# Direct 3x3 convolutions against minimal filtering F(4,3) along the rows, with filters streamed from HBM, in a convolution and attention block on one core

## The chip, the cores and the metric

The kernel runs on one core of a Trainium2 chip, in fp32. The metric is the device time of one launch in microseconds (us). TensorE is called PE in the profile, its weight loads PEld, VectorE is DVE, ScalarE is ACT, GpSimd is POOL and SyncE is SP.

## The reference

For each of 8 batch images of 512 channels x 32 x 32 the reference adds a block of convolutions and attention to the input:

```
t  = cbs(gn(x), cv1_w)            # 1x1, 512 -> 512, split into ys[0], ys[1] of 256 channels
for i in range(2):
    yi = ys[-1]
    z = cbs(yi, m_cv1_w[i])       # 3x3, 256 -> 256, zero padding of 1
    z = attention(z)              # q, k, v by 1x1; k + (rw + rh); softmax over 1024 positions, 4 heads of 64
    ys.append(yi + cbs(z, m_cv2_w[i]))          # 1x1, 256 -> 256
out = x + cbs(concat(ys), cv2_w)                # 1x1, 1024 -> 512
```

`gn` normalises over groups of 16 channels, `cbs` is a convolution, an affine step per channel (evaluation batch norm) and silu.

## The kernel before

Channels lie on the 128 partitions, in chunks of 128 (`NX` = 4 of the input, `NM` = 2 inside the block), and the 1024 positions along the free axis, in two halves of 512. The eight images are worked one after the other by written-out code; the order of the instructions on each engine is set by a scheduler of the framework, which follows the program's order and lets an instruction pass others whose inputs its own model expects later. Each image passes these stages:

- `gn_stats`, `gn_mean` and `gn_apply` (L205 to L238): statistics per channel on DVE, two small matmuls that average over groups, the power -0.5 on POOL (L228), and eight normalising operations on DVE (L233), which write the two `xn` tiles.
- `cv1` (L200 by `conv1x1`): four output chunks of 32 matmuls in the program in all; the first two go to `y0`, the last two to `ypad[0]`.
- `bottleneck(n)` for n = 0, 1: the 3x3 convolution (L432), `project` for q, k and v, `attention_fast`, the 1x1 convolution (L450), silu, and the sum with its input (L462). For n = 0 this sum is written to `ypad[1]`, which the second convolution reads.
- `cv2` (L200): four output chunks, silu, the sum with the input (L481) and the store by POOL's queue (L486).

silu is computed as (tanh(h) + 1) * h, where h is half of the affine step: `silu_parts` does the affine step on DVE out of PSUM (L183) and tanh on ACT (L184), and another DVE operation closes it (L191, L457, L480).

The 3x3 convolution reads `ypad[n]`, a tile with a border of zeros of 34 x 34 per chunk. For each of two output chunks (`oc`), two input chunks (`k`) and nine taps it issues two matmuls of 128 x 512, one per half. The filters `m1_sb` of both bottlenecks lie in SBUF from the start; they are loaded by ACT's queue. A program's fp32 matmul is two matmuls in the trace.

The PSUM pool `ps_big` has 3 tiles of two banks, `ps_av` 2 of one bank. Of the SBUF tag `pt` there are 3 tiles: `xn` and the exponentials of the attention take turns in them.

## Time and profile before

| | us |
|---|---|
| median of 3 runs | 3305.0 (3303.08 to 3305.64) |
| the profiled execution | 3307.59 |
| its span, first to last instruction | 3305.6 |
| PE busy in it | 3168.1 |
| DVE busy | 1490.6 |
| ACT busy | 763.3 |
| mean granted clock of PE in the span | 0.982 |

The busy times are sums over the span. PE's are modelled from the size of a matmul, and matmuls are pipelined; what one costs in a row of many is read from the start of the first and of what follows, over their count. An idle time counts only where the chain of work that ended last runs through it.

### The profile page before, as it was taken

To read this page: it belongs to the slowest core of one execution; us is meant where nothing else is said; L and a number is where in the kernel's file an instruction comes from. 1 tells how busy PE (TensorE), PEld (TensorE's weight loads), DVE (VectorE), ACT (ScalarE), POOL (GpSimd) and SP (SyncE) were. 2 spreads that over 40 slices of the span, in tenths; PEclk is the share of its full clock that TensorE was granted. 3 is DMA by queue.
4 is the path that set the end of the run, shared out by engine and by line. 5 is a ranking of instruction groups with operands and counts; after the bars stand their busy time and mean duration, and the time that the engine had idled before them with its cause. 6 is when DMAs were issued, how large, how long until landed. Compare 5 with 4: busy or idle time off the path is not lost.

```text
span 3305.6 us, 23035 instructions
## 1 busy us (share of the span) xinstructions
PE 3168.1 (96%) x9506; PEld 1303.5 (39%) x9506; DVE 1490.6 (45%) x1746; ACT 763.3 (23%) x961; POOL 57.3 (2%) x116
## 2 busy tenths in 40 slices
PE   6999999999999999999999999999999999999997
PEld 3434344343443434434444343443334333343333
DVE  2353633536335463444524455253552536516264
ACT  0222202222022320313103131031410404104040
POOL 1000000000000000000000000000000000000000
PEclk9999999999999999999999999999999999999999
DMA  4000000000000010000100001000010000100000
GB/s 154 1 0 0 26 26 0 0 0 26 26 0 0 0 37 14 0 0 1 38 13 1 0 0 39 13 0 0 1 51 1 0 0 0 45 0 0 0 0 27
DMA packets 14639, 45.23 MB, mean 14 GB/s; under 512 B 3264, under 2 KB 3776, under 8 KB 14016
## 3 DMA queue, kind: packets, MB, share of 16 engines
q1 hardware_dynamic: 4608, 16.78, 2.1%
q0 software_dynamic: 5632, 16.82, 1.3%
q10 hardware_dynamic: 4288, 10.09, 0.8%
q8 instruction: 77, 1.26, 0.2%
q14 instruction: 34, 0.28, 0.0%
HBM read 26.90 MB, written 16.78 MB: 13 GB/s over the span
## 4 chain that ended last, share of the span: by engine, by line
PE 77%; issue 13%; DVE 8%; DMA 1%; POOL 1%; ACT 0%; SPq 0%; DVEq 0%; POOLq 0%
PE c_ps L432 26%; PE ps L200 24%; PE l_ps L297 11%; PE av_ps L318 9%; DVE acc L307 3%; PE v_ps L268 3%; DVE rs L339 2%; PE m_ps L450 2%; PE s_ps L330 1%; DMA x<-in_x_dram 1%; DVE h L183 1%; DVE smin L338 0%; DVE rs L335 0%; ACT pt L301 0%; DVE t L457 0%
## 5 line engine op out<-in xcount | busy, mean ns | idle before, releaser
L432 PE MATMUL c_ps<-ypad,m_sb 128*128 128x512 f32 x2304 | 1013.8, 601 | 28.1 <-DVE ypad L462 27.1
L432 PEld LDWEIGHTS c_ps<-ypad,m_sb 128*128 128x128 f32 x2304 | 438.9, 191 | 601.7 <-issue 575.6
L301 ACT ACTIVATE pt<-l_ps 128x1024 f32<-128x1024 f32 x512 | 494.5, 1022 | 387.0 <-PE l_ps L297 387.0
L184 ACT ACTIVATE t<-h 128x512 f32<-128x512 f32 x256 | 161.3, 630 | 1794.5 <-DVE h L183 1785.9
L307 DVE TENSOR_TENSOR acc<-acc,pt 128x1024 f32<-128x1024 f32 x384 | 467.0, 1216 | 132.3 <-ACT pt L301 109.9
L297 PE MATMUL l_ps<-q,kr 64*128 64x512 f32 x2048 | 504.4, 613 | 0.0
L318 PE MATMUL av_ps<-pt,vT 128*64 128x512 f32 x2048 | 492.4, 604 | 0.0
L183 DVE TENSOR_SCALAR h<-c_ps,sh,bh 128x512 f32<-128x512 f32 x64 | 48.9, 805 | 910.1 <-PE c_ps L432 910.1
L297 PEld LDWEIGHTS l_ps<-q,kr 64*128 64x128 f32 x2048 | 177.6, 186 | 322.0 <-issue 314.5
L318 PEld LDWEIGHTS av_ps<-pt,vT 128*64 128x64 f32 x2048 | 125.6, 136 | 337.3 <-issue 264.1
L200 PE MATMUL ps<-xn,cv_sb 128*128 128x512 f32 x512 | 241.7, 636 | 15.9 <-DVE xn L233 15.9
L183 DVE TENSOR_SCALAR h<-ps,sh,bh 128x512 f32<-128x512 f32 x128 | 97.8, 805 | 286.8 <-PE ps L200 286.8
L200 PE MATMUL ps<-ypad,cv_sb 128*128 128x512 f32 x512 | 225.9, 592 | 0.0
L200 PE MATMUL ps<-z,qkv_sb 128*128 128x512 f32 x512 | 225.6, 593 | 0.0
L339 DVE RECIPROCAL rs<-rs 128x512 f32<-128x512 f32 x64 | 214.6, 3353 | 2.2
L200 PEld LDWEIGHTS ps<-xn,cv_sb 128*128 128x128 f32 x512 | 104.2, 205 | 147.5 <-issue 126.8
L200 PEld LDWEIGHTS ps<-ypad,cv_sb 128*128 128x128 f32 x512 | 96.6, 189 | 124.0 <-issue 124.0
L200 PEld LDWEIGHTS ps<-z,qkv_sb 128*128 128x128 f32 x512 | 95.9, 190 | 117.8 <-issue 99.5
L304 DVE TENSOR_TENSOR acc<-pt 128x1024 f32<-128x1024 f32 x64 | 78.4, 1225 | 107.8 <-ACT pt L301 107.8
L259 DVE TENSOR_TENSOR kr<-ps,rw_sb 128x512 f32<-128x512 f32 x64 | 41.2, 686 | 188.6 <-PE ps L200 188.6
L450 PE MATMUL m_ps<-ao,m_sb 128*128 128x512 f32 x256 | 117.6, 602 | 2.9 <-DVE ao L341 2.9
L200 PE MATMUL ps<-y,cv_sb 128*128 128x512 f32 x256 | 116.4, 592 | 0.0
(70 smaller groups left out, 1313.1 us busy)
## 6 DMA issues: line engine op xcount, KB each, us to landing
x<-in_x_dram SPq DMA_DIRECT2D x32, 512.0 KB, 4.3
out_dram<-t POOLq DMA_DIRECT2D x64, 256.0 KB, 2.5
m_sb<-in_m_cv_w_dram ACTq DMA_DIRECT2D x2, 2304.0 KB, 13.4
cv_sb<-in_cv_w_dram ACTq DMA_DIRECT2D x1, 2048.0 KB, 14.4
qkv_sb<-in_m_qkv_w_dram ACTq DMA_DIRECT2D x2, 768.0 KB, 15.5
cv_sb<-in_cv_w_dram ACTq DMA_DIRECT2D x1, 1024.0 KB, 8.9
m_sb<-in_m_cv_w_dram ACTq DMA_DIRECT2D x2, 256.0 KB, 10.7
bnp<-in_cv_bn_dram POOLq DMA_DIRECT2D x8, 2.0 KB, 6.4
```

Of the source, the lines that this page charges most:

```text
L183: nc.vector.tensor_scalar(h, ps, sh[:, k : k + 1], bh[:, k : k + 1], ALU.mult, ALU.add)
L184: nc.scalar.activation(t, h, AF.Tanh)
L200: nc.tensor.matmul(ps[:, half, :], w_of(k), rhs_of(k, half), start=(k == 0), stop=(k == nk - 1))
L268: nc.tensor.matmul(ps[:, j, :], z[:, k, ts(j0 + j, P)], qkv_sb[:, n, k, 2 * C : 3 * C], start=(k == 0), stop=(k == NM - 1),)
L297: nc.tensor.matmul(ps[:, hd, :], kr[r, c, ts(j, P)], q[r, c, ts(half, HALF)], start=True, stop=True,)
L301: nc.scalar.activation(pt[:, i], ps, AF.Exp, scale=SCALE)
L304: nc.vector.tensor_tensor(accs[g], pt[:, 0], pt[:, 1], ALU.add)
L307: nc.vector.tensor_tensor(accs[g], accs[g], pt[:, i], ALU.add)
L318: nc.tensor.matmul(avs[g][hd * HD : (hd + 1) * HD, :], vT[:, j, o : o + HD], pt[:, i, hd, :], start=(j == 0), stop=(j == NJ - 1),)
L339: nc.vector.reciprocal(rs, rs)
L432: nc.tensor.matmul(ps[:, half, :], m1_sb[:, n, k, tap, ts(oc, P)], yi[:, k, r0 : r0 + ROWS, dx : dx + F], start=(k == 0 and tap == 0), sto ...
L450: nc.tensor.matmul(pss[oc][:, half, :], m2_sb[:, n, k, ts(oc, P)], ao[:, k, ts(half, HALF)], start=(k == 0), stop=(k == NM - 1),)
```

## The change

The direct 3x3 convolution is replaced by minimal filtering F(4,3) along the rows' axis of the image: four output rows come from six transformed input rows, so that each of 3 column taps needs six products in place of twelve. There are 8 tiles of four rows, so a matmul has 8 x 32 = 256 columns, and the matmuls of one output chunk are 6 positions x 2 chunks x 3 column taps.

- Once, at the start: each filter chunk (`raw`) is loaded by SP's queue, combined on DVE and ACT into six sets (`u_new`), and stored to HBM by POOL's queue. Raw and combined filters share four buffers (tag `u`).
- For each convolution four tiles of combined filters are loaded by SP's queue into the same four buffers (L522 of the changed kernel). `m1_sb` and its loads go.
- `rows_in` builds the six transformed sets of one input chunk in a tile `v_in` of the tag `pt` (DVE, with two POOL fills for the border columns); `ypad` keeps its border rows only.
- `rows_out` turns six product sets into four rows: a copy on ACT, the rest on DVE. Positions 1 to 4 are accumulated in `c3_mid`, of `ps_big`; 0 and 5 in `c3_end`, of `ps_av`. The scale 1/24 is folded into the affine step's factor.
- In `silu_parts` the affine step goes from DVE to ACT. After the 3x3 convolution, tanh is taken with the affine step inside it, and a DVE operation in SBUF does the affine step for the closing product.
- The general path, which runs only if a softmax sum leaves its range, gets smaller buffers.

```diff
-    m1_sb = const.tile([P, N, NM, 9, C], F32, name="m1_sb")
-        nc.scalar.dma_start(m1_sb[:, n], m_cv1_w[n].rearrange("(k p) t o -> p k t o", p=P))
-        yp = const.tile([P, NM, F + 2, F + 2], F32, name=f"ypad{n}")
+        yp = const.tile([P, NM, F + 2, F], F32, name=f"ypad{n}")
...
+    for at in bn_m1:
+        nc.vector.tensor_scalar(sh[:, at : at + NM], sh[:, at : at + NM], 1 / 24, None, ALU.mult)
+    for n in range(N):
+        for k in range(NM):
+            raw = const.tile([P, 9, C], F32, tag="u", name="raw", bufs=4)
+            nc.sync.dma_start(raw, m_cv1_w[n, ts(k, P)])
+            for oc in range(NM):
+                g0, g1, g2 = (raw[:, 3 * r : 3 * r + 3, ts(oc, P)] for r in range(3))
+                u = const.tile([P, NPOS, 3, P], F32, tag="u", name="u_new", bufs=4)
+                tmp = act.tile([P, 3, 3, P], F32, tag="pt", name="u_tmp", bufs=3)
+                even, odd, wide = tmp[:, 0], tmp[:, 1], tmp[:, 2]
+                nc.scalar.mul(u[:, 0], g0, 6.0)
+                nc.scalar.mul(u[:, 5], g2, 24.0)
+                nc.scalar.mul(odd, g1, -4.0)
+                nc.vector.tensor_tensor(even, g0, g2, ALU.add)
+                nc.vector.scalar_tensor_tensor(u[:, 1], even, -4.0, odd, ALU.mult, ALU.add)
+                nc.vector.scalar_tensor_tensor(u[:, 2], even, -4.0, odd, ALU.mult, ALU.subtract)
+                nc.vector.scalar_tensor_tensor(wide, g2, 4.0, g0, ALU.mult, ALU.add)
+                nc.vector.scalar_tensor_tensor(u[:, 3], g1, 2.0, wide, ALU.mult, ALU.add)
+                nc.vector.scalar_tensor_tensor(u[:, 4], g1, -2.0, wide, ALU.mult, ALU.add)
+                nc.gpsimd.dma_start(u_dram[n][oc][k], u)
...
         def silu_parts(ps, k):
-            nc.vector.tensor_scalar(h, ps, sh[:, k : k + 1], bh[:, k : k + 1], ALU.mult, ALU.add)
+            nc.scalar.activation(h, ps, AF.Identity, scale=sh[:, k : k + 1], bias=bh[:, k : k + 1])
             nc.scalar.activation(t, h, AF.Tanh)
...
+        def rows_in(yp, k):
+            v = act.tile([P, NPOS, NT, F + 2], F32, tag="pt", name="v_in", bufs=n_pt)
+            nc.gpsimd.memset(v[:, :, :, 0:1], 0.0)
+            nc.gpsimd.memset(v[:, :, :, F + 1 : F + 2], 0.0)
+            tmp = act.tile([P, 3, NT, 2, F], F32, tag="wt", name="w_tmp", bufs=1)
...
+            nc.vector.scalar_tensor_tensor(
+                flat(ba), flat(rows(1, 2)), -4.0, flat(rows(3, 2)), ALU.mult, ALU.add
+            )
+            nc.vector.tensor_tensor(flat(ec), flat(rows(3, 2)), flat(rows(1, 2)), ALU.subtract)
+            nc.vector.tensor_tensor(g, rows(0, 2, 5), rows(2, 2), ALU.subtract)
...
+            tt(to(1), a_, b_, ALU.add)
+            tt(to(2), a_, b_, ALU.subtract)
+            stt(to(3), e_, 2.0, c_, ALU.mult, ALU.add)
+            stt(to(4), e_, -2.0, c_, ALU.mult, ALU.add)
+            stt(to(0), g0, 4.0, c_, ALU.mult, ALU.add)
+            stt(to(5), e_, -4.0, g1, ALU.mult, ALU.add)
+            return v
+        def rows_out(dst, mid, end):
+            m24 = act.tile([P, 2, NT * F], F32, tag="rs", name="m24", bufs=2)
+            nc.scalar.copy(m24, mid[:, 1::2, :])
+            sd = act.tile([P, 2, 2, NT * F], F32, tag="acc", name="sd", bufs=2)
+            nc.vector.tensor_tensor(sd[:, :, 0], mid[:, 0::2, :], m24, ALU.add)
+            nc.vector.tensor_tensor(sd[:, :, 1], mid[:, 0::2, :], m24, ALU.subtract)
+            s_, d_, big_s, big_d = sd[:, 0, 0], sd[:, 0, 1], sd[:, 1, 0], sd[:, 1, 1]
+            ends = act.tile([P, 2, NT * F], F32, tag="rs", name="ends", bufs=2)
+            nc.vector.tensor_tensor(ends, end, sd[:, 0], ALU.add)
...
+            nc.vector.tensor_tensor(to(0), tiles(ends[:, 0]), tiles(big_s), ALU.add)
+            stt(to(1), tiles(big_d), 2.0, tiles(d_), ALU.mult, ALU.add)
+            stt(to(2), tiles(big_s), 4.0, tiles(s_), ALU.mult, ALU.add)
+            stt(to(3), tiles(big_d), 8.0, tiles(ends[:, 1]), ALU.mult, ALU.add)
...
         def bottleneck(n, attend):
+            vs = [rows_in(yi, k) for k in range(NM)]
             for oc in range(NM):
+                us = []
                 for k in range(NM):
-                    for tap in range(9):
...
+                    u = const.tile([P, NPOS, 3, P], F32, tag="u", name="u", bufs=4)
+                    nc.sync.dma_start(u, u_dram[n][oc][k])
+                    us.append(u)
+                mid = ps_big.tile([P, 4, NT * F], F32, tag="big", name="c3_mid")
+                end = ps_av.tile([P, 2, NT * F], F32, tag="av", name="c3_end")
+                for pos in (1, 2, 3, 4, 0, 5):
+                    dst = mid[:, pos - 1, :] if 0 < pos < 5 else end[:, pos // 5, :]
+                    for i in range(NM * 3):
+                        k, dx = divmod(i, 3)
+                        nc.tensor.matmul(
+                            dst, us[k][:, pos, dx, :], vs[k][:, pos, :, dx : dx + F],
+                            start=(i == 0), stop=(i == NM * 3 - 1),
+                        )
+                rows_out(z[:, oc, :], mid, end)
+                k = bn_m1[n] + oc
                 for half in range(NH):
+                    part = z[:, oc, ts(half, HALF)]
+                    nc.scalar.activation(t, part, AF.Tanh, scale=sh[:, k : k + 1], bias=bh[:, k : k + 1])
+                    nc.vector.tensor_scalar(
+                        part, part, sh[:, k : k + 1], bh[:, k : k + 1], ALU.mult, ALU.add
+                    )
+                    nc.vector.scalar_tensor_tensor(part, t, 1.0, part, ALU.add, ALU.mult)
```

The order of the instructions shows four places. Lines in the following rows are those of the changed kernel, where the row is one of the change.

PE, the first convolution of the first image, in the change, after the last matmul of `cv1`. `v_in_378` is the transformed chunk 0, `v_in_391` chunk 1; `c3_mid_408` and `c3_end_409` belong to output chunk 0, `c3_mid_469` and `c3_end_470` to output chunk 1. Before, one row of 72 matmuls of 128 x 512 in the order of the loops stood here.

```order
L530 MATMUL c3_mid_408<-v_in_378,u_404 128x256 x3
L530 MATMUL c3_end_409<-v_in_378,u_404 128x256 x3
L530 MATMUL c3_mid_469<-v_in_378,u_465 128x256 x3
L530 MATMUL c3_end_470<-v_in_378,u_465 128x256 x3
L530 MATMUL c3_mid_408<-v_in_391,u_406 128x256 x3
L530 MATMUL c3_mid_408<-v_in_378,u_404 128x256 x3
L530 MATMUL c3_mid_408<-v_in_391,u_406 128x256 x3
```

Four sets of three matmuls on chunk 0, two of them of output chunk 1, stand ahead of the first on chunk 1. In the second convolution three matmuls of `c3_mid` and two of `c3_end` do. Behind a convolution, PE's order has four projection matmuls of 512 columns on chunk 0 and one of 256 (L360) before the first on chunk 1.

DVE, from the end of the first bottleneck to the second convolution, in the change (`w_tmp` and `v_in` are `rows_in`'s, L254 to L270). Before, L183, L457 and L462 of the four pieces stood here, and then the L183 that follows the convolution.

```order
L562 SCALAR_TENSOR_TENSOR t<-t,h 128x512
L567 TENSOR_TENSOR ypad_120<-t,ypad_115 128x512
L562 SCALAR_TENSOR_TENSOR t<-t,h 128x512
L254 SCALAR_TENSOR_TENSOR w_tmp<-ypad_120 128x512
L567 TENSOR_TENSOR ypad_120<-t,ypad_115 128x512
L257 TENSOR_TENSOR w_tmp<-ypad_120 128x512
L258 TENSOR_TENSOR w_tmp<-ypad_120 128x512
L265 TENSOR_TENSOR v_in<-w_tmp 128x8x32
L266 TENSOR_TENSOR v_in<-w_tmp 128x8x32
```

The first operation of `rows_in` on chunk 0 stands ahead of the last sum; all others, and those on chunk 1, behind it. In the first convolution of an image all nine operations on chunk 0 stand ahead of the closing silu operations of `cv1`'s last output chunk.

DVE, the start. Before, the normalising operations (L233) came directly behind the statistics. In the change:

```order
L187 TENSOR_TENSOR u_tmp<-raw 128x384
L188 SCALAR_TENSOR_TENSOR u_new<-u_tmp 128x384
L189 SCALAR_TENSOR_TENSOR u_new<-u_tmp 128x384
L191 SCALAR_TENSOR_TENSOR u_new<-raw,u_tmp 128x384
L192 SCALAR_TENSOR_TENSOR u_new<-raw,u_tmp 128x384
L188 SCALAR_TENSOR_TENSOR u_new<-u_tmp 128x384
L189 SCALAR_TENSOR_TENSOR u_new<-u_tmp 128x384
L190 SCALAR_TENSOR_TENSOR u_tmp<-raw 128x384
L325 TENSOR_SCALAR xn<-x,gm,gr 128x512
L191 SCALAR_TENSOR_TENSOR u_new<-raw,u_tmp 128x384
L192 SCALAR_TENSOR_TENSOR u_new<-raw,u_tmp 128x384
L325 TENSOR_SCALAR xn<-x,gm,gr 128x512 x7
```

Of the 48 operations on filters, 46 stand ahead of the first normalising operation, L325.

DVE, from one image to the next: first before, then in the change.

```order
L183 TENSOR_SCALAR h<-ps,sh,bh 128x512 x2
L480 SCALAR_TENSOR_TENSOR t<-t,h 128x512
L217 COPY gm<-gm_ps 128x4
L481 TENSOR_TENSOR t<-t,x 128x512
L480 SCALAR_TENSOR_TENSOR t<-t,h 128x512
L218 TENSOR_TENSOR dev<-mv,gm 128x4
L481 TENSOR_TENSOR t<-t,x 128x512
L219 TENSOR_TENSOR dev<-dev 128x4
L220 TENSOR_TENSOR dev<-dev,mv 128x4
L227 TENSOR_SCALAR gr<-gv_ps 128x4
L233 TENSOR_SCALAR xn<-x,gm,gr 128x512 x8
```

```order
L309 COPY gm<-gm_ps 128x4
L310 TENSOR_TENSOR dev<-mv,gm 128x4
L311 TENSOR_TENSOR dev<-dev 128x4
L312 TENSOR_TENSOR dev<-dev,mv 128x4
L319 TENSOR_SCALAR gr<-gv_ps 128x4
L325 TENSOR_SCALAR xn<-x,gm,gr 128x512 x2
L585 SCALAR_TENSOR_TENSOR t<-t,h 128x512 x2
L586 TENSOR_TENSOR t<-t,x 128x512 x2
L325 TENSOR_SCALAR xn<-x,gm,gr 128x512 x6
```

The small operations of the statistics and two normalising ones have moved ahead of the closing operations of the last output chunk, L585 and L586 (L480 and L481 before).

## Rows read from the trace of the kernel before

**Rows 1.** The page, part 1: busy us (share of the span), instructions.

```profile
PE 3168.1 (96%) x9506; PEld 1303.5 (39%) x9506; DVE 1490.6 (45%) x1746; ACT 763.3 (23%) x961; POOL 57.3 (2%) x116
```

**Rows 2.** The page, part 4: shares of the chain that ended last, by engine and line.

```profile
PE 77%; issue 13%; DVE 8%; DMA 1%; POOL 1%; ACT 0%; SPq 0%; DVEq 0%; POOLq 0%
PE c_ps L432 26%; PE ps L200 24%; PE l_ps L297 11%; PE av_ps L318 9%; DVE acc L307 3%; PE v_ps L268 3%; DVE rs L339 2%; PE m_ps L450 2%; PE s_ps L330 1%; DMA x<-in_x_dram 1%; DVE h L183 1%; DVE smin L338 0%; DVE rs L335 0%; ACT pt L301 0%; DVE t L457 0%
```

**Rows 3.** The chain in order of time: start us, us, engine, tile, line, count.

```profile
435.94 30.30 PE ps L200 x64
466.24 61.83 PE c_ps L432 x144
528.07 6.91 PE ps L200 x16
534.98 6.91 PE v_ps L268 x32
...
627.60 62.69 PE c_ps L432 x140
...
1037.06 60.37 PE c_ps L432 x140
```

**Rows 4.** Groups by line and shape: busy us, mean ns | idle us before, releaser.

```profile
L307 DVE TENSOR_TENSOR acc<-acc,pt 128x1024 f32<-128x1024 f32 x384 | 467.0, 1216 | 132.3 <-ACT pt L301 109.9 <-DVE acc L307 0.9
...
L184 ACT ACTIVATE t<-h 128x512 f32<-128x512 f32 x256 | 161.3, 630 | 1794.5 <-DVE h L183 1785.9
...
L268 PEld LDWEIGHTS v_ps<-qkv_sb,z 128*128 128x128 f32 x512 | 97.3, 190 | 20.1 <-issue 7.7
...
L183 DVE TENSOR_SCALAR h<-c_ps,sh,bh 128x512 f32<-128x512 f32 x64 | 48.9, 805 | 910.1 <-PE c_ps L432 910.1
...
L191 DVE SCALAR_TENSOR_TENSOR z<-t,h 128x512 f32<-128x512 f32 x64 | 44.3, 692 | 1.8
...
L254 ACT COPY q<-ps 128x512 f32<-128x512 f32 x64 | 34.4, 589 | 167.2 <-PE ps L200 167.2
L233 DVE TENSOR_SCALAR xn<-x,gm,gr 128x512 f32<-128x512 f32 x64 | 29.9, 541 | 9.5 <-POOL gr L228 9.5
```

**Rows 5.** Waits of TensorE: us in total, times, longest us.

```profile
PE c_ps L432 <- DVE ypad L462: 27.1, 16, 2.4
```

**Rows 6.** Timeline, second convolution of batch 0: start us, us, instruction [idle before].

```profile
210.38 1.98 PE L450 MATMUL m_ps<-ao,m_sb 128*128 128x512 f32 x4 [0.36 <-DVE ao L341]
...
211.54 1.67 DVE L183 TENSOR_SCALAR h<-m_ps,sh,bh 128x512 f32<-128x512 f32 x2 [1.22 <-PE m_ps L450]
...
218.56 3.78 PE L432 MATMUL c_ps<-ypad,m_sb 128*128 128x512 f32 x4 [0.57 <-DVE ypad L462]
```

**Rows 7.** Windows there: busy us by engine, then granted clock, DMA share, GB/s.

```profile
218.00:220.00 2.00, 1.44 (x2) 0.84 (x3) 1.80 (x3) 0.00 (x0) 0.00 (x0) 0.50 0.00 0
```

**Rows 8.** Timeline, from the last output matmuls to the next batch.

```profile
428.76 1.53 DVE L183 TENSOR_SCALAR h<-ps,sh,bh 128x512 f32<-128x512 f32 x2 [3.19 <-PE ps L200]
...
433.12 0.16 DVE L220 TENSOR_TENSOR dev<-dev,mv 128x4 f32<-128x4 f32 x1
...
435.94 4.63 PE L200 MATMUL ps<-xn,cv_sb 128*128 128x512 f32 x5 [1.95 <-DVE xn L233]
```

**Rows 9.** Timeline at the start, a window there, and the page's input transfers.

```profile
17.56 1.29 DVE L208 BATCH_NORM_STATS2 st<-x 128x6 f32<-128x512 f32 x2 [3.39 <-DMA x<-in_x_dram]
...
26.86 3.74 DVE L233 TENSOR_SCALAR xn<-x,gm,gr 128x512 f32<-128x512 f32 x8 [1.13 <-POOL gr L228]
...
20.00:30.00 10.00, 3.12 (x5) 1.67 (x6) 5.58 (x19) 1.28 (x1) 3.94 (x2) 1.00 1.05 396
...
x<-in_x_dram SPq DMA_DIRECT2D x32, 512.0 KB, 4.3
```

More of the change, by code (lines that the diff above doesn't have):

```diff
@@ L75 @@
     SCALE = HD**-0.5
+    NPOS = 6
+    NT = F // 4
     const = ctx.enter_context(tc.tile_pool(name="const", bufs=1))
@@ L162 @@
     nc.vector.scalar_tensor_tensor(bh, bnp[:, :, 1], 0.5, bh, ALU.mult, ALU.subtract)
+    for at in bn_m1:
+        nc.vector.tensor_scalar(sh[:, at : at + NM], sh[:, at : at + NM], 1 / 24, None, ALU.mult)
+    u_dram = [
+        [[tc.dram_tile([P, NPOS, 3, P], F32, name=f"u{n}{oc}{k}") for k in range(NM)] for oc in range(NM)]
+        for n in range(N)
+    ]
+    for n in range(N):
[17 more added lines that the diff above has]
+                nc.gpsimd.dma_start(u_dram[n][oc][k], u)
     NSUM = B * N * NM * NH
@@ L173, in inner @@
     def inner(yp, c, half):
-        return yp[:, c, 1 + half * ROWS : 1 + (half + 1) * ROWS, 1 : F + 1]
+        return yp[:, c, 1 + half * ROWS : 1 + (half + 1) * ROWS, :].rearrange("p h w -> p (h w)")
     def stages(act, small, ps_big, ps_av, n_pt):
@@ L203, in conv1x1, with rows, flat, to @@
             return ps
+        def rows_in(yp, k):
[3 more added lines that the diff above has]
+            tmp = act.tile([P, 3, NT, 2, F], F32, tag="wt", name="w_tmp", bufs=1)
+            y = yp[:, k]
+            def rows(a, n=1, step=1):
+                return bass.AP(
+                    tensor=y.tensor, offset=y[:, a : a + 1, :].offset,
+                    ap=[y.ap[0], [4 * F, NT], [step * F, n], [1, F]],
+                )
+            def flat(ap):
+                return ap.rearrange("p t a w -> p t (a w)")
+            ba, ec, g = tmp[:, 0], tmp[:, 1], tmp[:, 2]
+            nc.vector.scalar_tensor_tensor(
[3 more added lines that the diff above has]
+            nc.vector.tensor_tensor(g, rows(0, 2, 5), rows(2, 2), ALU.subtract)
+            def to(pos):
+                return v[:, pos, :, 1 : F + 1]
+            stt, tt = nc.vector.scalar_tensor_tensor, nc.vector.tensor_tensor
+            b_, a_, e_, c_, g0, g1 = ba[:, :, 0], ba[:, :, 1], ec[:, :, 0], ec[:, :, 1], g[:, :, 0], g[:, :, 1]
+            tt(to(1), a_, b_, ALU.add)
[5 more added lines that the diff above has]
+            return v
@@ L364, in attention_general @@
                     sums = small.tile([P, NIC, 2], F32, tag="sums", name="sums")
-                    pts = [act.tile([P, NJ, IB], F32, tag="gpt", name="gpt", bufs=2) for _ in range(2)]
+                    pts = [act.tile([P, NJ, IB], F32, tag="pt", name="gpt", bufs=n_pt) for _ in range(2)]
                     for ic in range(NIC):
@@ L458, in bottleneck @@
                     if n == N - 1:
-                        dst = img(ylast[:, oc, ts(half, HALF)])
+                        dst = ylast[:, oc, ts(half, HALF)]
                     else:
                         dst = inner(ypad[n + 1], oc, half)
-                    nc.vector.tensor_tensor(dst, img(t), inner(yi, oc, half), ALU.add)
+                    nc.vector.tensor_tensor(dst, t, inner(yi, oc, half), ALU.add)
             return ylast
```

23 lines of the change are left out of this document (8 added, 15 removed).

## The prediction

> **What bounds the kernel now.** I read the busy times first, then the chain of work that ended last, then the same chain in order of time. TensorE is busy for 96% of the span and VectorE for 45% [rows 1]. In the chain 77% is TensorE, and the largest single line is the 3x3 convolution, L432 [rows 2]. In order of time a batch is an almost unbroken run of TensorE: the first 1x1 stage (64 matmuls), the convolution (144 matmuls in 61.83 us), the projections, the attention, and again from the second convolution on [rows 3]. So TensorE's columns are the bound, and what is taken from them is worth its full time, as long as the new vector work finds cover. One matmul of 128x512 in the program is two in the trace; the convolution's pitch is 61.83/144 = 429 ns. The 256-column matmuls of L268 already show the pitch at half the columns: 32 in 6.91 us, 216 ns [rows 3].
>
> **The convolution.** Before, one convolution is 2 x 2 x 9 x 2 = 72 matmuls of 512 columns. Now it is 2 output chunks x 6 positions x 6 (chunk, dx) = 72 matmuls of 256 columns, again 144 in the trace. 144 x 216 ns = 31.1 us against 61.83, so 30.7 us for each of 16 convolutions: 492 us if nothing comes in between. The moving operand keeps its row pitch of 34, which the old one had too.
>
> The weight loads: L268 loads weights once for every 256-column matmul, one load takes 190 ns [rows 4], and still 32 matmuls take 32 x 216 ns, so the load lies beneath the matmul. [...]
>
> Prices for VectorE: 512 elements take 692 ns (L191), 1024 take 1216 (L307) [rows 4]. On that line 256 elements cost 430 ns and 384 cost 561. One call of rows_in is 3 operations of 512 and 6 of 256: 3 x 0.69 + 6 x 0.43 = 4.66 us, two calls per convolution. For ScalarE's new affine step the nearest row is its PSUM copy, 589 ns (L254); tanh is 630 (L184) [rows 4].
>
> *Entry of the first convolution of a batch.* Before there is no gap: 435.94 + 30.30 = 466.24 [rows 3]. Now VectorE does rows_in of chunk 0 while TensorE still computes the last chunk of the 1x1 stage (6.9 us), and TensorE has 12 matmuls of chunk 0 (four sets of three, two of them for the other output chunk) before it needs chunk 1: 12 x 0.432 = 5.2 us. Chunk 1 comes after two affine steps and two tanh on ScalarE, one closing silu, three operations of 512 and one of 256: 2.0 us to the first tanh, then 2 x 0.69 + 3 x 0.69 + 0.43, which is 5.9 us after the stage ends. Exposed: about 0.8 us. The convolution takes 31.9 us, a gain of 29.9; 8 times, 239 us.
>
> *Entry of the second.* Here the input is the sum at the end of the first bottleneck, and nothing else is left to do. Before, the silu of the four pieces starts at 211.54, the convolution runs from 218.56 [rows 6] for some 62.4 us (62.69 in the next batch [rows 3]), until 281.0. Now ScalarE needs 4 x (0.59 + 0.63) = 4.9 us, to 216.4; VectorE closes the last silu (217.1), does the first operation of rows_in, the last addition and two more of 512 (219.9), six of 256 (222.5), then three of 512 and one of 256 for chunk 1 (225.0). Only 5 matmuls run meanwhile; 67 are left, 28.9 us, to 254.1. [...] I charge that again: 256.4, a gain of 24.5; 8 times, 196 us. TensorE waited 27.1 us in total here before [rows 5].
>
> *Exit.* After its last matmul the convolution now needs one addition of 512, two operations of 256, tanh, an affine step of 541 ns (L233 is that operation in SBUF [rows 4]) and 692 ns: 0.69 + 0.86 + 0.63 + 0.54 + 0.69, with handovers some 3.9 us, until half 0 of the second chunk is there, and 1.2 more for half 1. TensorE's order has four matmuls and one of 256 columns on chunk 0 first, 3.9 us, then two on half 0, 1.7 us. I charge 0.3 us, 16 times: 5 us. Its bounds are 0 and 2.3 us each, the latter if TensorE could only use the two matmuls of one projection (1.7 us) as cover. The first half of the inverse transform lies beneath the last 12 matmuls of its chunk.
>
> **The affine step on ScalarE** takes 805 ns off VectorE per half (L183 [rows 4]) and puts about 590 on ScalarE, which is 23% busy [rows 1]. Inside the stages its cover is the matmuls of the next chunk (6.9 or 13.8 us). It matters where the next batch's normalisation waits: from the last output matmul (428.7, just before L183 begins) to the first matmul of the next batch (435.94) pass 7.2 us [rows 8], and the affine steps and closing operations of L480 and L481 stand between the statistics on VectorE. In the new order the statistics come first. From the operation L220 to TensorE's start it takes 435.94 - 433.28 = 2.7 us; with some 1.0 us before it the gap is about 3.6 us. The rest of the normalisation waits 2.8 us behind four closing operations, and the matmuls on the first two pieces cover it. Gain 3.6 us, 7 times: 25 us. At the end of the program it is a loss of 0.4 us.
>
> **The start.** VectorE's first normalising operation, at 26.86 us [rows 9], now stands behind all but two of 48 filter operations. They cannot start before the filters land, which are queued behind the first four input tiles; the statistics of the fourth begin at 17.56 [rows 9]. From some 17.5 us 48 x 0.561 = 26.9 us give 44 us as the lower bound: +17. The tiles also pass through a ring of four buffers (12 tiles of 1,152 KB): a load or a store of one takes between 3.1 us (at the 396 GB/s of the first stage) and 9.7 us (at 512 KB in 4.3 us for one transfer [rows 9]), and about five such hops lie in a row after the first load. Five at 3.1 us, with four blocks of arithmetic of 3.4 us, from some 21 us give 50; at 9.7 us, 72 or more. So +17 to +45; the transfers share the bandwidth but rarely run alone, so I take +25.
>
> **The stream.** Four filter tiles per convolution, 4.6 MB, are 38.7 us at the lower rate. Their issue waits for the previous convolution's matmuls, and from the end of one convolution to the start of the next pass 627.60 - 528.07 = 99.5 us [rows 3], more over a batch's end. SP's queue holds the inputs of the next batch behind the next four filter tiles, and those are free to go some 100 us before the inputs are wanted. Price 0; without cover, 38.7 us each.
>
> **Sum:** 239 + 196 - 5 + 25 - 0.4 - 25 = 430 us. The profiled execution took 3307.6 us, 2.6 above the median of 3305.0; the same 430 off the median gives 2,875 us.
>
> **Rivals.**
> - *The clock.* Each new short wait lets the granted clock fall: 2.3 us more at 8 first entries and 16 exits, 55 us, and the shorter gap between batches gives nothing, 25 us: 2,955 us. For it: the old gap of 2.4 us and a second small one did it in most batches. Against: the new waits are below 1 us. Chance 0.14.
> - *No cover.* The two calls of rows_in and the exit lie bare in all convolutions: 9.3 + 4.6 = 13.9 us, where the sum holds 1.1 at the first and 6.5 at the second of a batch: 8 x 12.8 + 8 x 7.4 = 162 us, 3,037 us. The order of instructions speaks against it. Chance 0.10.
> - *Weight loads come to the surface:* with half the columns over a load, 190 of 216 ns are needed; if loads do not run beneath these matmuls, 2304 x 190 ns = 438 us come back: 3,313 us, slower. It decides from 187 ns per matmul on. L268 shows the opposite. Chance 0.03. [...]
> - *The stream is bare:* 16 x 38.7 = 619 us, 3,494 us, slower; it decides from 26.9 us per convolution. Chance 0.02.
> - *More gain:* the start at its lower bound (8 us), no low clock at the second entries (18 us) and after the shorter gaps between batches (64 matmuls in 30.30 instead of 27.5 us, 2.8 us, 7 times): 2,829 us at best. Chance 0.07.
>
> My forecast, 2,850 to 2,920 us, has 0.64. The range from 2,835 to 2,990 us leaves out the bare transforms, the two slower cases and the very best one. Less than 0.2%, 6.6 us, could not be told from no change. Faster 0.95: all but the two slower cases, of which 0.01 may end within 0.2%; slower 0.04.
>
> **What would show it.** 144 matmuls of a convolution in some 31 us at a pitch of 216 ns; under 1 us of waiting at first entries and some 12 us, 5 matmuls in it, at second ones; about 0.3 us at the projections; a gap of 3 to 4 us between batches; the first 1x1 matmul at 45 to 72 us; no TensorE wait on a DMA after the first batch. A pitch near 400 ns, waits on filter tiles, or a TensorE idle for 10 us at each entry would make it wrong.

## The result, and the profile after

The changed kernel takes 2859.1 us (median of 4 runs, 2858.7 to 2861.5) against 3305.3 us before in the same session: a ratio of 0.865, 95% interval 0.864 to 0.867. That is 446 us less; the forecast was 430 less, 2,875 us. The span of the profiled execution is 2857.4 us against 3305.6, 448 us less. In the lines below L530 is the 3x3 convolution, L229 the 1x1 convolutions, L214 the affine step of silu, L265 the first of six 256-element operations of `rows_in`, L325 the normalisation.

The page, parts 1 and 4 (busy time, and the chain that ended last), to be held against [rows 1, 2]:

```profile
PE 2670.4 (93%) x9506; PEld 1308.0 (46%) x9506; DVE 1582.2 (55%) x2116; ACT 923.6 (32%) x1209; POOL 72.0 (3%) x180
...
issue 56%; PE 37%; DVE 3%; POOL 1%; DMA 1%; ACT 0%; POOLq 0%; DVEq 0%; ACTq 0%; SPq 0%
```

TensorE has the same number of matmuls, lost 498 us of busy time and is still busy for 93% of the span. VectorE gained 92 us and ScalarE 160. The chain now runs for 56% through pieces that it calls issue. The longest, of some 164 us each, are not TensorE's (the chain in order of time, batch 1):

```profile
548.80 0.21 POOL v_in L239
549.01 163.85 issue
...
712.88 0.54 POOL out_dram L591
```

Such a piece lies on GpSimd's queue, between a border fill and a store, and TensorE waits 8.33 us within this one (the second convolution, below). So the shares of this chain do not tell what bounds the kernel now. That TensorE still does, but for the start and the entries shown below, is read from its 93% and from its waits.

The page's groups of the convolution and of the moved affine step (busy us, mean ns, idle before):

```profile
L530 PE MATMUL c_mid<-v_in,u 128*128 128x256 f32 x1536 | 354.2, 388 | 70.7 <-DVE v_in L265 66.6
L530 PEld LDWEIGHTS c_mid<-v_in,u 128*128 128x128 f32 x1536 | 297.8, 195 | 127.1 <-issue 83.7
...
L214 ACT ACTIVATE h<-ps,bh,sh 128x512 f32<-128x512 f32 x128 | 92.5, 773 | 521.5 <-PE ps L229 521.5
```

A load shows 195 ns, where L268's showed 190 [rows 4]. The affine step out of PSUM takes 773 ns on ScalarE, where 590 had been charged from the copy.

The chain in order of time, first 1x1 stage of batches 0, 1 and 2 (start us, us):

```profile
57.04 29.76 PE ps L229 x64
...
405.25 29.50 PE ps L229 x64
...
753.31 29.40 PE ps L229 x64
```

A batch takes 753.31 - 405.25 = 348.1 us; before it was 845.27 - 435.94 = 409.3 in the same chain that [rows 3] are from. Over 7 steps that is 429 us. The first matmul comes 29.6 us later: TensorE starts 0.6 us behind the first normalising operation, which stood at 26.86 [rows 9] and stands at 56.45 now.

TensorE's waits after the change (us in total, times, longest):

```profile
PE c_mid L530 <- DVE v_in L265: 66.6, 8, 8.3
PE ps L229 <- DVE xn L325: 48.1, 8, 33.8
...
PE c_mid L530 <- issue: 4.1, 8, 0.5
```

No line of this view names a DMA. The first one is the second convolution of each batch, against 27.1 us in 16 waits before [rows 5]; the second holds the start; the third is the first convolution of each batch.

**First convolution of a batch.** TensorE's timeline in batch 1 (start us, us, instruction, count, idle before); chunk 0 is used alone until 439.9:

```profile
434.59 1.46 PE L530 MATMUL c_mid<-v_in,u 128*128 128x256 f32 x6
...
438.48 1.46 PE L530 MATMUL c_end<-v_in,u 128*128 128x256 f32 x6
440.45 9.30 PE L530 MATMUL c_mid<-v_in,u 128*128 128x256 f32 x42 [0.51 <-issue]
...
466.42 3.60 PE L229 MATMUL ps<-z,qkv_sb 128*128 128x512 f32 x8
```

From 434.59 to 466.42 are 31.8 us, with 0.51 us of waiting; 31.9 and 0.8 were forecast. Less the wait it is 31.3/144 = 217 ns for a matmul.

**Second convolution of a batch.** The timeline of ScalarE, VectorE and TensorE in batch 1:

```profile
558.08 1.99 PE L555 MATMUL m_ps<-ao,m_sb 128*128 128x512 f32 x4 [0.36 <-DVE ao L433]
559.25 0.78 ACT L214 ACTIVATE h<-m_ps,bh,sh 128x512 f32<-128x512 f32 x1 [8.41 <-PE m_ps L555]
...
567.73 0.41 DVE L265 TENSOR_TENSOR v_in<-w_tmp 128x256 f32<-128x256 f32 x1
568.06 0.42 DVE L266 TENSOR_TENSOR v_in<-w_tmp 128x256 f32<-128x256 f32 x1
...
568.40 2.90 PE L530 MATMUL c_mid<-v_in,u 128*128 128x256 f32 x6 [8.33 <-DVE v_in L265]
...
571.67 0.42 DVE L265 TENSOR_TENSOR v_in<-w_tmp 128x256 f32<-128x256 f32 x1
...
572.80 1.43 PE L530 MATMUL c_mid<-v_in,u 128*128 128x256 f32 x5
```

And the windows there (after the busy times of PE, PEld, DVE, ACT, POOL: granted clock, DMA share, GB/s):

```profile
565.00:572.00 7.00, 3.60 (x9) 2.92 (x10) 6.97 (x15) 0.00 (x0) 0.00 (x0) 0.50 0.00 0
572.00:602.00 30.00, 30.00 (x138) 26.19 (x137) 9.51 (x21) 2.69 (x4) 0.00 (x0) 0.98 0.22 83
```

TensorE waits 8.33 us. Ten matmuls on chunk 0 then run at a granted clock of 0.50 and take 4.4 us. Chunk 1's first set is written at 572.09 (571.67 + 0.42), 3.7 us into them and 0.7 us before the first matmul on it. From 572.80 on the other 134 take until 601.90, 217 ns each, at a granted clock of 0.98 in the second window. From the first affine step to the end pass 42.7 us, against 69.4 before (211.54 [rows 6] to 281.0) and 44.9 forecast. ScalarE's four pieces come first, one every 1.33 us from 559.25 on; behind them VectorE is busy for 6.97 of the 7 us from 565.00 on. The two chains in a row set this entry.

**From one image to the next:**

```profile
401.63 0.28 PE L306 MATMUL gm_ps<-mv,gmat 128*128 128x4 f32 x2
...
404.56 1.00 DVE L325 TENSOR_SCALAR xn<-x,gm,gr 128x512 f32<-128x512 f32 x2 [1.15 <-POOL gr L320]
405.25 5.04 PE L229 MATMUL ps<-xn,cv_sb 128*128 128x512 f32 x7 [2.04 <-DVE xn L325]
405.48 1.28 DVE L585 SCALAR_TENSOR_TENSOR t<-t,h 128x512 f32<-128x512 f32 x2
```

The gap is 3.6 us, as forecast, against some 7.2 [rows 8]. The closing operations (L585) now start when TensorE has its first two pieces.

**The exit** of the first convolution:

```profile
469.63 0.69 DVE L543 SCALAR_TENSOR_TENSOR z<-t,z 128x512 f32<-128x512 f32 x1
469.86 0.59 PE L360 MATMUL v_ps<-qkv_sb,z 128*128 128x256 f32 x2
...
470.38 3.70 PE L229 MATMUL ps<-z,qkv_sb 128*128 128x512 f32 x8
```

Two matmuls of 216 ns from 469.86 end at 470.29; the next, which need half 0, start at 470.38: 0.1 us, not 0.3.

**The start.** VectorE's filter work, with what ended its idle time, and a window there:

```profile
33.85 0.56 DVE L188 SCALAR_TENSOR_TENSOR u_new<-u_tmp 128x384 f32<-128x384 f32 x1 [3.22 <-DMA u<-u_new]
...
44.01 0.56 DVE L187 TENSOR_TENSOR u_tmp<-raw 128x384 f32<-128x384 f32 x1 [7.60 <-DMA raw<-in_m_cv_w_dram]
...
56.45 0.54 DVE L325 TENSOR_SCALAR xn<-x,gm,gr 128x512 f32<-128x512 f32 x1
```

```profile
30.00:57.00 27.00, 0.00 (x0) 0.00 (x0) 14.31 (x31) 6.22 (x14) 2.65 (x5) 1.00 0.91 354
```

The normalisation waits behind filter operations that wait for tiles, with the DMA engines at 0.91 and TensorE at nothing.

### The profile page after: what moved, and what is told of

Same layout as the page of the kernel before. It is cut to its first block, busy times and chain, and to the rows that moved or that the text cites. A ratio compares the mean times of both kernels' runs of the same rounds, so it can differ in the third digit from the quotient of the medians.

```text
span 2857.4 us, 24013 instructions
## 1 busy us (share of the span) xinstructions
PE 2670.4 (93%) x9506; PEld 1308.0 (46%) x9506; DVE 1582.2 (55%) x2116; ACT 923.6 (32%) x1209; POOL 72.0 (3%) x180
## 4 chain that ended last, share of the span: by engine, by line
issue 56%; PE 37%; DVE 3%; POOL 1%; DMA 1%; ACT 0%; POOLq 0%; DVEq 0%; ACTq 0%; SPq 0%
PE ps L229 12%; PE l_ps L389 7%; PE av_ps L410 6%; PE c_mid L530 6%; PE c_end L530 3%; PE v_ps L360 2%; DVE acc L399 1%; DVE rs L431 1%; POOL out_dram L591 1%; PE s_ps L422 0%; DMA raw<-in_m_cv_w_dram 0%; DMA bnp<-in_cv_bn_dram 0%; DMA u<-u_new 0%; ACT pt L393 0%; POOL gr L320 0%
## 5 line engine op out<-in xcount | busy, mean ns | idle before, releaser
L530 PE MATMUL c_mid<-v_in,u 128*128 128x256 f32 x1536 | 354.2, 388 | 70.7 <-DVE v_in L265 66.6
L530 PEld LDWEIGHTS c_mid<-v_in,u 128*128 128x128 f32 x1536 | 297.8, 195 | 127.1 <-issue 83.7
L229 PE MATMUL ps<-xn,cv_sb 128*128 128x512 f32 x512 | 236.2, 624 | 48.1 <-DVE xn L325 48.1
L214 ACT ACTIVATE h<-ps,bh,sh 128x512 f32<-128x512 f32 x128 | 92.5, 773 | 521.5 <-PE ps L229 521.5
L229 PE MATMUL ps<-z,qkv_sb 128*128 128x512 f32 x512 | 229.2, 595 | 0.0
L229 PE MATMUL ps<-ypad,cv_sb 128*128 128x512 f32 x512 | 224.9, 592 | 0.0
L530 PE MATMUL c_end<-v_in,u 128*128 128x256 f32 x768 | 181.9, 389 | 0.0
L229 PEld LDWEIGHTS ps<-xn,cv_sb 128*128 128x128 f32 x512 | 100.0, 198 | 178.3 <-issue 119.4
L530 PEld LDWEIGHTS c_end<-v_in,u 128*128 128x128 f32 x768 | 149.9, 195 | 22.6
L229 PEld LDWEIGHTS ps<-ypad,cv_sb 128*128 128x128 f32 x512 | 97.3, 190 | 122.5 <-issue 122.5
L279 DVE TENSOR_TENSOR sd<-c_mid,m 128x512 f32<-128x512 f32 x32 | 22.1, 691 | 228.3 <-ACT m L277 228.3
L229 PEld LDWEIGHTS ps<-z,qkv_sb 128*128 128x128 f32 x512 | 95.9, 190 | 106.5 <-issue 95.7
L585 DVE SCALAR_TENSOR_TENSOR t<-t,h 128x512 f32<-128x512 f32 x64 | 41.3, 687 | 171.2 <-ACT t L215 171.2
L277 ACT COPY m<-c_mid 128x512 f32<-128x512 f32 x32 | 18.7, 585 | 347.8 <-PE c_mid L530 347.8
## 6 DMA issues: line engine op xcount, KB each, us to landing
cv_sb<-in_cv_w_dram ACTq DMA_DIRECT2D x1, 2048.0 KB, 13.5
```

Of the source, the lines that this page charges most:

```text
L214: nc.scalar.activation(h, ps, AF.Identity, scale=sh[:, k : k + 1], bias=bh[:, k : k + 1])
L229: nc.tensor.matmul(ps[:, half, :], w_of(k), rhs_of(k, half), start=(k == 0), stop=(k == nk - 1))
L530: nc.tensor.matmul(dst, us[k][:, pos, dx, :], vs[k][:, pos, :, dx : dx + F], start=(i == 0), stop=(i == NM * 3 - 1),)
L585: nc.vector.scalar_tensor_tensor(t, t, 1.0, h, ALU.add, ALU.mult)
```

## The experiments

All times are medians beside runs of the kernel before on the same chip (3306 to 3307 us); "after" is the changed kernel, 2859.1 us, measured beside 3305.3. A difference of 1 or 2 us is therefore not read as one.

**1. The affine step back on VectorE, in the changed kernel.**

```diff
-            nc.scalar.activation(h, ps, AF.Identity, scale=sh[:, k : k + 1], bias=bh[:, k : k + 1])
+            nc.vector.tensor_scalar(h, ps, sh[:, k : k + 1], bh[:, k : k + 1], ALU.mult, ALU.add)
```

> The changed kernel with the affine step of silu_parts back on VectorE. Theory (VectorE's queue ends the waits at two places, and the affine step lengthens both): between batches the gap goes from 3.6 back to 7.2 us and the first 1x1 stage from 29.5 to 30.3 us, 7 times 4.4 = 31 us; at the entry of the second convolution VectorE is busy without a pause, so most of 4 x 0.72 us shows, about 2.5 us, 8 times = 20 us; together about 2,910 us. Rival (the affine step lies beneath TensorE, ScalarE or VectorE alike, and the whole gain is the convolution's): 2,855 to 2,865 us.

Measured: 2891.3 us, ratio 0.875 (0.873 to 0.876), 32 us more than after. TensorE's waits:

```profile
PE c_mid L530 <- DVE v_in L265: 77.9, 8, 9.7
...
PE gv_ps L317 <- DVE dev L312: 39.0, 8, 6.8
```

In batch 5 the last matmul before the gap (L306) starts at 2165.70 and the next batch at 2173.07: 7.4 us instead of 3.6, times 7 is 26. The second entry waits 1.4 us longer, of which the clock gives some back: from the last four matmuls of m_ps (L555) to the last 24 of the convolution pass 39.3 us instead of 38.7, 5 us in 8 batches. The 1x1 stage behind the gap, expected to be longer in every batch, is so in two of the seven (30.7 instead of 29.5 us). Both places are where the theory put them; the size was overrated.

**2. The affine step alone on ScalarE, in the kernel before.** The edit of experiment 1 the other way round, on L183.

> The kernel before with the affine step on ScalarE and nothing else changed. Theory: the gap between batches goes from 7.2 to 3.6 us and the first 1x1 stage loses 0.8 us less to the clock, 7 times 4.4 = 31 us; the entry of the second convolution is paced by ScalarE's 1.33 us a piece and gains at most 0.3 us; about 3,272 us. Rival (no part of the gain is the affine step's): 3,300 to 3,310 us. If the two parts add up, this and the run with the affine step back on VectorE together bound the part of the convolution alone.

Measured: 3256.9 us, ratio 0.985 (0.983 to 0.987): 49 us less, more than expected. From one batch to the next and at the second convolution of batch 4 TensorE's timeline reads:

```profile
2035.58 29.40 PE L200 MATMUL ps<-xn,cv_sb 128*128 128x512 f32 x64 [2.11 <-DVE xn L233]
...
2224.88 60.37 PE L432 MATMUL c_ps<-ypad,m_sb 128*128 128x512 f32 x140 [0.61 <-DVE ypad L462]
```

The gap before the first row is 3.7 us, and the 64 matmuls behind it take 29.4 us at a granted clock of 0.94, where [rows 3] have 30.30 at 0.91; but two of the seven later batches take 30.6 to 30.7 us here too. At the second convolution the time from the last matmuls of m_ps to the run of 140 is 6.8 us instead of 8.2 in the same batch before, and such a run takes 60.4 us in five batches, where before had 62.4 to 62.7 in six of eight. From the first matmul of each stage to that of the next, over all batches, the gaps give 26 us, the second convolutions with their entries 22 and the 1x1 stages 3; the end of the program takes 2 back. The second entry and its clock are what the expectation left out. The two parts overlap: 49 us by this and 415 by experiment 1 would be 464; both at once give 446, since in the changed kernel the affine step is worth 32 and not 49.

**3. No stream:** the four filter tiles are loaded once and kept; the second bottleneck uses the filters of the first, so its own are left out.

```diff
-                us = []
-                for k in range(NM):
+                us = held_u.get(oc, [])
+                for k in range(NM - len(us)):
```

> The changed kernel with the four filter tiles of the first bottleneck loaded once and kept; both bottlenecks of all batches multiply by them (the second bottleneck's own filters are left out after they are combined and stored). The start is the same. Theory (the stream is wholly hidden): 2,855 to 2,863 us. Rival (the loads slow other work by sharing SBUF or delay the next batch's inputs): 15 us or more less, below 2,845 us.

Measured: 2859.2 us, ratio 0.865 (0.863 to 0.866), no difference. The main hardware queue falls from 97.0 to 26.2 MB. The stream costs nothing here.

**4. Chunk 1 first:** the matmuls of each position begin with the chunk whose transform comes last.

```diff
-                        k, dx = divmod(i, 3)
+                        k, dx = NM - 1 - i // 3, i % 3
```

> The changed kernel with the matmuls of each position on chunk 1 first, then on chunk 0, so that nothing can run while chunk 1 is transformed. Theory (the 12 and the 5 matmuls on chunk 0 are real cover): TensorE waits some 5.2 us more at the first convolution of a batch and some 2.2 us more at the second, 8 x 7.4 = 59 us, about 2,918 us, with up to 2.3 us more per first entry where the clock falls (18 us). Rival (the wait is as long whatever stands ahead): 2,855 to 2,870 us.

Measured: 2946.9 us, ratio 0.891 (0.890 to 0.893), 88 us more. TensorE's timeline, first and second convolution of batch 5:

```profile
2246.36 11.98 PE L530 MATMUL c_mid<-v_in,u 128*128 128x256 f32 x48 [5.84 <-DVE v_in L265]
...
2384.66 12.80 PE L530 MATMUL c_mid<-v_in,u 128*128 128x256 f32 x48 [12.11 <-issue]
```

The waits are 5.84 us instead of 0.51 and 12.11 instead of 8.33, and the first run of 48 behind each takes 1.5 and 2.3 us more than the 10.5 of later ones, at a granted clock of 0.88 and 0.83 where those have 1.00. In the changed kernel the ten slow matmuls of the second entry already lose 2.2 us that way (4.4 us for ten pitches of 217 ns), so the second entry pays more in waiting alone and the first in both: together 10.6 us a batch, 85 in 8, more than the 59 to 77 expected. So the matmuls on chunk 0 are the cover, and an entry without it can cost waiting and clock. The kernel's granted clock falls from 0.979 to 0.969.

**5. Late filters:** the filters of the first bottleneck are combined behind the first normalisation in the program, those of the second behind the first bottleneck; the helper tile moves to another tag.

```diff
+    xn = s.gn_apply(*s.gn_mean(mv), xs)
+    filters(0)
...
+            if b == 0 and n == 1:
+                filters(1)
             ylast = s.bottleneck(n, lambda n, z: s.attention_fast(n, z, at))
```

> The changed kernel with the filters of the first bottleneck combined behind the first normalisation in the program's order, and those of the second behind the first bottleneck. Theory (the start is lost because the normalisation stands behind all filter work on VectorE's queue): the first 1x1 matmul at 27 to 29 us in place of 57.0, the first convolution's filters there in time, 25 to 30 us less: about 2,831 us. Rival (the first convolution cannot start earlier, since its filters pass through HBM and the ring of buffers first): the wait moves to the first convolution, 2,850 to 2,862 us.

Measured: 2828.2 us, ratio 0.856 (0.854 to 0.857), 31 us less than after. TensorE's first 1x1 stage:

```profile
25.23 30.07 PE L229 MATMUL ps<-xn,cv_sb 128*128 128x512 f32 x64 [1.93 <-DVE xn L325]
```

The first matmul is at 25.2 us instead of 57.0. The filters are ready when the convolution wants them (no wait on a DMA there), so the whole cost of the start was one of order. Before the change the first 1x1 matmul stood at 27.47 us.

**6. Two calls of rows_in interleaved**, so that the first sets of chunk 1 come before the last of chunk 0.

```diff
-            vs = [rows_in(yi, k) for k in range(NM)]
+            parts = [rows_in(yi, k) for k in range(NM)]
+            vs = [next(p) for p in parts]
+            for p in parts:
+                list(p)
```

> The changed kernel with the two calls of rows_in interleaved: for each chunk the three operations of 512 and the first position, then the rest (the second chunk's temporary lies in another buffer). Theory (VectorE ends the wait at the second convolution, 0.335 us for each of the five operations moved): chunk 1's first position comes 1.7 us earlier, and three matmuls instead of five run ahead of it, so 0.8 us less, 8 times = 6 us; 2,853 us. Rival (the wait there is ScalarE's four silu pieces, not VectorE): no difference, 2,859 us.

Measured: 2860.6 us, ratio 0.865 (0.864 to 0.867): nothing. A miss. At the second entry of batch 1 chunk 1's first set is written at 569.97, 1.9 us behind TensorE's first matmul instead of 3.7, and TensorE goes on to chunk 1 after six matmuls instead of ten. But the window of its first ten, whichever chunk they read, is as long as before:

```profile
568.08:572.48 4.40, 4.40 (x10) 3.51 (x11) 4.40 (x12) 0.00 (x0) 0.00 (x0) 0.50 0.01 2
```

The granted clock is 0.50 in it, with no wait: what the earlier data could have given, the low clock takes. The entry itself still stands where chunk 0 puts it (a wait of 8.34 us).

**7. Both edits, 5 and 6.**

> Late filters and interleaved transforms together. Theory (they act at different places, so they add up): 28 + 6 = 34 us less than the changed kernel, about 2,825 us. Rival (what the start gives is lost later): 2,850 us or more.

Measured: 2828.9 us, ratio 0.856 (0.854 to 0.857), the time of experiment 5.

**8. Matmuls of 128 columns:** each of 256 is cut in two, so that twice as many loads stand over the same columns.

```diff
-                    for i in range(NM * 3):
+                    for j in range(2 * NM * 3):
+                        q, i = divmod(j, NM * 3)
...
-                            dst, us[k][:, pos, dx, :], vs[k][:, pos, :, dx : dx + F],
+                            dst[:, ts(q, P)], us[k][:, pos, dx, :],
+                            vs[k][:, pos, q * NT // 2 : (q + 1) * NT // 2, dx : dx + F],
```

> The changed kernel with each 256-column matmul cut into two of 128 columns, each with its own weight load: the same columns, twice the loads. Theory (a load of some 195 ns runs beneath a matmul, and a matmul of 216 ns just covers it): now the load sets the pitch, 288 x 0.195 = 56 us per convolution in place of 31.1, 16 x 25 = 400 us more, about 3,260 us. Rival (loads and matmuls do not overlap): 288 x (0.108 + 0.195) = 87 us, about 3,755 us. Rival (loads cost nothing at any width): 2,859 us.

Measured: 2913.8 us, ratio 0.881 (0.880 to 0.883): 55 us more, where loads in the way of matmuls would have made some 400. The load's group and TensorE's timeline in batch 1:

```profile
L531 PEld LDWEIGHTS c_mid<-v_in,u 128*128 128x128 f32 x3072 | 370.5, 202 | 102.4 <-issue 102.2
```

```profile
447.83 11.91 PE L531 MATMUL c_mid<-v_in,u 128*128 128x128 f32 x90 [3.02 <-issue]
459.59 4.85 PE L531 MATMUL c_end<-v_in,u 128*128 128x128 f32 x42
464.28 10.21 PE L531 MATMUL c_mid<-v_in,u 128*128 128x128 f32 x90
474.33 4.85 PE L531 MATMUL c_end<-v_in,u 128*128 128x128 f32 x42
```

From 464.28 to 474.33 are 90 matmuls: 112 ns each, with one load of 202 ns listed for every one. So loads, as listed, lie beneath matmuls and beneath each other. The pitches at 512, 256 and 128 columns, each with a load, are 429, 217 and 112 ns: twice 112 is only 7 ns more than 217, and twice 217 only 5 more than 429, so a load that lay bare could not take more than some 5 to 7 ns. The 55 us are elsewhere: in this order only the first half of the columns on chunk 0 stands ahead of chunk 1, 2.7 us of cover instead of 5.2, so the wait is 3.02 us instead of 0.51, and the run behind it takes 11.8 us at a granted clock of 0.86 where the later one takes 10.05 at 1.00; 288 pitches of 112 against 144 of 216 ns are 1.1 us. That is 5.3 us in the first convolution; the 1x1 stage (30.6 instead of 29.5 us; why is not shown) and the second convolution add 1.5; 8 times 6.8 is 54.

**9. Rows ahead** (on top of experiment 5): between the bottlenecks the silu pieces go chunk by chunk, and chunk 0's transform stands directly behind its two sums.

```diff
+                pieces.sort(key=lambda p: p[1])
...
+                    if n_pt == 3 and n < N - 1 and half == NH - 1:
+                        ahead.append(rows_in(ypad[n + 1], oc))
```

> The version with late filters (2828.2 us), and between the bottlenecks the four silu pieces go chunk by chunk, with the transform of chunk 0 directly behind the two sums of chunk 0. Theory (the wait of 8.3 us at the second entry ends with chunk 0, but what TensorE then has on chunk 0 is 10 matmuls only): chunk 0 is there two pieces (2.7 us) earlier, the 10 matmuls take 4.3 us at the low clock, and then TensorE waits for chunk 1, which comes at the same time as now or some 0.7 us earlier. So the listed wait for chunk 0 falls from 8.3 to about 5.7 us, a new one of about 1.5 us for chunk 1 appears, and the time falls by 0 to 8 us: 2820 to 2828. Rival (chunk 0 alone sets the entry): 8 x 2.7 us less, about 2807.

Measured: 2838.2 us, ratio 0.858 (0.857 to 0.859): 10 us more than experiment 5. The timeline shows a side effect, in the first batch alone:

```profile
215.01 2.90 PE L532 MATMUL c_mid<-v_in,u 128*128 128x256 f32 x6 [33.76 <-DMA u<-u]
```

The filters of the second bottleneck had slid behind the transform of chunk 1 on VectorE, and TensorE waits 33.8 us for them. The later batches take 345.4 to 346.7 us instead of 348.1.

**10. Three sums open** (on top of experiment 5): one accumulation per PSUM bank is kept open for three positions, chunk 0 first, so that 18 matmuls on chunk 0 stand ahead at the second entry instead of 10.

```diff
+                trios = ((1, 3, 0), (2, 4, 5)) if n_pt == 3 else tuple((p,) for p in (1, 2, 3, 4, 0, 5))
+                for trio in trios:
+                    for k, pos, dx in [(k, pos, dx) for k in range(NM) for pos in trio for dx in range(3)]:
```

> The version with late filters (2828.2 us), and three sums are kept open at a time (one per PSUM bank), so that 18 matmuls on chunk 0 stand ahead of the first on chunk 1 in the second convolution instead of 10, and 26 instead of 24 in the first. Theory: at the second entry nothing changes, since chunk 1 is there when the 10 matmuls end; at the first entry 0.43 of the 0.51 us of waiting go, 8 times, 3.5 us: about 2825. Rival (the order of the matmuls costs or gives nothing anywhere): 2828.

Measured: 2846.7 us, ratio 0.861 (0.860 to 0.862): 18 us more than experiment 5, so both theories missed. The entry is as expected (no wait at the first convolution any more, 8.3 us at the second), but TensorE's waits have a new line:

```profile
PE ps L229 <- DVE z L543: 19.3, 16, 3.4
```

Positions 2, 4 and 5 now end together, so the first half of the inverse transform, which needs 1 to 4, no longer lies beneath the last 12 matmuls of its chunk. In batch 2 it begins 0.4 us before the convolution ends (790.24 and 790.66), after the change 3.0 us (463.41 and 466.42), and the projections wait 1.05 us.

**11. Experiments 9 and 10 together.**

> Both edits: chunk 0 two pieces earlier, and 18 matmuls on chunk 0 to fill the time until chunk 1 is there (18 x 0.22 to 0.43 us = 3.9 to 7.8 us against some 5.6 us between the two chunks). Theory: 2.7 us at each of 8 second entries, less up to 1.7 us where the clock is back early and the 18 end before chunk 1 is there, and 3.5 us at the first entries: 2803 to 2817. Rival (VectorE's whole chain up to chunk 1 sets the entry, or the clock falls for longer): no more than the first entries' 3.5 us, about 2825.

Measured: 2855.8 us, ratio 0.864 (0.862 to 0.865). A miss as well: the two costs of experiments 9 and 10 add up, the wait on a filter tile (33.1 us) and the exits (17.0), and outweigh the earlier start.

**12. Rows ahead, with the second filters combined behind the first attention.**

> The run with rows ahead, with one thing put back: the filters of the second bottleneck are combined behind the first attention, ahead of the silu pieces in the program, so that they no longer stand behind the transform of chunk 1. Theory (chunk 0 alone sets the second entry; the 33.8 us that one TensorE wait on a filter transfer took in the first batch of that run hid it): the batch period is 345.4 us there against 348.06, so 8 x 2.7 = 21 us less than the version with late filters: 2805 to 2812, and no wait on a filter tile. Rival (the earlier start is given back at chunk 1 or by a lower clock in most batches): 2820 to 2828.

Measured: 2811.5 us, ratio 0.850 (0.849 to 0.852): the fastest version, within what was expected, 48 us below the changed kernel and 17 below experiment 5. TensorE's waits and its second convolution in batch 3:

```profile
PE c_mid L532 <- DVE v_in L265: 49.6, 8, 6.2
```

```profile
1217.13 1.98 PE L557 MATMUL m_ps<-ao,m_sb 128*128 128x512 f32 x4 [0.36 <-DVE ao L433]
1225.31 2.90 PE L532 MATMUL c_mid<-v_in,u 128*128 128x256 f32 x6 [6.19 <-DVE v_in L265]
...
1258.34 1.88 PE L229 MATMUL ps<-z,qkv_sb 128*128 128x512 f32 x4
```

From 1217.13 to 1258.34 are 41.2 us instead of 43.8 (558.08 to 601.90). The wait is 2.1 us shorter, 17 us in 8 batches. The order had also changed on TensorE: 20 matmuls on chunk 0 run before the long run that begins at 1231.50, so the earlier start is not given back at chunk 1.

## Why the prediction was right, point by point

- **The convolution** (144 x 216 ns): right, 217 measured. The load beneath the matmul, read from L268, holds with more room than the prediction saw. Its rival had "190 of 216 ns" as the margin, and experiment 8 runs at 112 ns with a load of the same size, listed with 202 ns, for each matmul.
- **First entry:** 0.8 us forecast, 0.51 measured; the gain is 30.0 instead of 29.9, 240 us. Experiment 4 shows that its cover is the matmuls on chunk 0.
- **Second entry:** the mis-sized term. It was to take 44.9 us from the first affine step and takes 42.7. The step that failed is the 2.3 us charged again for a low clock. They are the difference of two runs of 140 before, 62.69 and 60.37 us [rows 3], and the granted clock was 0.50 at this entry of batch 0 [rows 7]; the profile of the changed kernel does not show them as time lost. The granted clock is 0.50 there too, but during ten matmuls that mostly have to wait for chunk 1 anyway, so that at most 0.7 us of it shows; the 134 behind them run at 217 ns. Experiment 6 is the other side of it: with chunk 1 there earlier, the low clock counts in full and nothing is gained. The rest is the chain ahead of chunk 1's first set, charged 13.5 us from the first affine step and measured 12.8: ScalarE's price was 0.18 us too low a piece, and VectorE's too high (below); these nearly cancel. Not every batch before paid 2.3 us, so the gain is about 26 us, 209 in 8 batches instead of 196.
- **Exit:** 0.3 us charged, 0.1 found; 1.6 us in all instead of 5.
- **Affine step and the gap:** 3.6 us forecast, 3.6 measured; measured alike in all 7 gaps, 26 us. The sum left out the clock of the 1x1 stage behind the gap, which only the rival "more gain" has: 29.4 to 29.5 us instead of 30.03 to 30.44, at a granted clock of 0.94 instead of 0.91 in batch 1, another 6 us. Experiments 1 and 2 price the whole step at 32 us in the changed kernel and 49 in the old.
- **The start:** 25 us charged between bounds of 17 and 45, 29.6 measured. The picture of hops through four buffers is in the rows (33.85, 44.01), and experiment 5 shows all of it to be avoidable.
- **The stream:** price 0, confirmed by experiment 3.
- **End of the program:** 0.4 us charged, 1.9 found, from the last matmul of the batches to the end of the span (2838.66 to 2857.4, and 3288.72 to 3305.6 before).

The terms as measured: 240 + 209 + 26 + 6 - 29.6 - 1.6 - 1.9 = 448 us, as the spans differ. The sum was 18 us short; the second entry, the 1x1 stage's clock and the exit gave some 22 more than charged and the start and the end took 6 more, so a part of the nearness is cancelling. Of the rivals, the clock did the opposite of what was feared, since shorter gaps gave a part of it back; bare transforms, bare loads and a bare stream are answered by experiments 4, 8 and 3. That ScalarE's step weighs 773 instead of 590 ns shows in the chain at both entries, but VectorE's operations in that chain took less than charged.

Three figures of the prediction do not follow from its own terms: 225.0 and 28.9 give 253.9, not 254.1; 1,152 KB at 396 GB/s are 3.0 us, not 3.1; and from 21 us five hops of 9.7 us with four blocks of 3.4 give 83 us as the upper bound of the start, not 72. None of them decided anything.

## What to carry to other kernels

When work moves from TensorE to an engine beside it, count for each hand-over what stands ahead in TensorE's order that does not need the new operand: here the matmuls on chunk 0 were the difference between 0.5 and 5.8 us of waiting at the first entry, and a matmul order that covers the entry better can bare the exit (experiment 10: 19.3 us of waits in 16 exits). Put one-time preparation behind what the first stage needs, and look again at where it lands after every edit: the filter operations cost 30 us, nothing, or 34 us by their place in the order alone. A clock loss is worth a charge only for the time in which the slow matmuls are not waiting for data anyway: at the second entry ten matmuls lost 2.2 us at a granted clock of 0.50, and at most 0.7 of it showed. Data that come earlier may only uncover it: in experiment 6 chunk 1's first set was there 1.9 us behind the first matmul instead of 3.7, and the time stayed at 2860.6 us.
